# Expert rows filled in rounds, the residual kept on chip, and result gathers ahead of the last routing, in a graph-attention and mixture-of-experts kernel

## The chip, the cores and the metric

The kernel runs on one core of a Trainium2 chip. Its time is the device time of one execution in microseconds (us). Verdicts on two kernels come from runs of both on the same chip.

The engines named below are TensorE (PE; its weight loads are PEld), VectorE (DVE), ScalarE (ACT), GpSimd (POOL) and SyncE (SP). SyncE, ScalarE and GpSimd also issue DMAs; a queue's own instructions have a q behind the name (SPq, ACTq).

## The reference

6250 nodes of 256 values go through a graph-attention layer (8 heads of 32) over 206,250 edges, which are sorted by destination, and then through a mixture of 16 experts of which each node takes two. Both have a residual and a layer norm. Cut to what matters:

```python
h = layernorm(x)
hh = (h @ W).reshape(n, 8, 32)
scores = leaky_relu(s_src[src] + s_dst[dst], 0.2)
alpha = softmax of scores over the edges of one dst
out = segment_sum(hh[src] * alpha, dst) + h
x = x + elu(layernorm(out) * gamma + beta)

y = layernorm(x)
topk_vals, topk_idx = top_k(y @ gate_w + gate_b, 2)
topk_w = softmax(topk_vals)
h = relu(y @ w1[e] + b1[e])
expert_out = h @ w2[e] + b2[e]
moe = sum over the two experts of topk_w * expert_out
x = x + layernorm(y + moe) * gamma + beta
```

## The kernel before

Nodes are handled in 49 blocks of 128. A first stage norms the nodes, multiplies them by W, and writes a table in DRAM with one row of 280 fp32 values a node: 8 heads of 32 values and a one, and the exponentials of its source score. Everything after it happens in one loop, with a tail.

**The edge loop.** The edges are cut into 52 chunks (`k`) of 31 tiles of 128 edges, and each chunk into groups of 8, 8, 8 and 7 tiles (`GROUPS`). For a group:

- GpSimd issues one indirect DMA a tile (`gather`, L188), which fetches the 128 table rows of the tile's sources into a buffer `hx`. The pool has four such buffers, so four groups can be ahead.
- VectorE builds two one-hot matrices of the edges' places among the destinations, `oh` (L864) and `ohT` (L871). TensorE multiplies `ohT` by the destination scores `abw` (L879), into `pm`.
- VectorE folds `pm` (`uv`, L887), multiplies by the source part (L890), takes the larger of two forms (L892) and weighs the rows of `hx` (L895).
- TensorE sums the weighed rows by destination, one product pair a tile (L898), into `agg`. An `hx` buffer is free when its last sum has been made.

At the end of a chunk the last sums are carried into the next (L910, L912) and sent to DRAM (`accd`, L914). SyncE fetches `abw` and the row of places `dlr` two chunks ahead (`fetch`).

**Node blocks.** When a chunk has completed the sums of a block, `node_block` reads them back, norms, applies the elu, adds x, norms again into `acc[:, b, :]`, which stays in SBUF, and computes the gate's logits and their two largest. The residual of the block (`res`, L580) goes out to DRAM (`resd`, L581).

**Parts.** Blocks are gathered into five parts that end at 14, 26, 35, 43 and 49 (`PARTS`). When a part's last block is done, `routing` computes, for each node and each of its two experts, the row in the part's DRAM buffer `xg` at which it stands (`pos`), with each expert's rows filled up to a multiple of 128, and for each tile of 128 rows its expert (`owner`). A part of n blocks needs up to 2n + 15 tiles, 173 in all. GpSimd then scatters the blocks' rows into `xg` (`scatter`, L709), two indirect DMAs a block. `biases` multiplies the routing's shares (`shares`) by the experts' second biases and adds the product to `acc`.

**Expert tiles.** A tile passes through four steps, one a call of `some()`, which is called after each group: `weights` (SyncE reads the expert's number into a register and fetches the tile's rows `xr` L736, `w1s` L738, `b1s` L740), `turned` (fetches `w2s` L745, transposes the rows L749), `hidden` (16 products L758, ReLU on ScalarE L767) and `rows_out` (8 products L773, a copy L775, and a DMA into `yg` L776). `some()` also takes up to four scatters, or one block's biases.

**The tail.** After the last chunk the queues are emptied, and then `result` is called for each block: it gathers its two rows from `yg` (L787, ordered behind the last scatter), adds them with their gates to `acc` (L793), norms, reads the residual back (`res`) and writes the output (L800, L801).

**What sets the order.** The kernel is written with a tile framework, which assigns buffers, adds the waits and places the instructions of each engine in an order of its own making; `tc.issue_after` forces one instruction behind another. On the chip each engine takes its queue in that order. Buffers of a pool are used in turn, and most small products of the parts and of `routing` share one PSUM bank, the tag `pt`.

The lines that call the stages at the end of a chunk:

```python
            for b in when.get(k, ()):
                node_block(b)
                for i, (lo, hi) in enumerate(parts):
                    if b == hi - 1:
                        part_due(i)
```

## Time and profile before

| what | value |
| --- | --- |
| median of 3 runs | 2642.37 us (2632.72 to 2643.17) |
| the profiled execution | 3281.45 us |
| its span, first to last instruction | 3279.4 us |
| TensorE's mean granted clock | 0.796 of full speed |
| first gather's place on GpSimd's queue, last gather | 90.7 us, 2894.0 us |
| bytes read from and written to HBM | 504.0 MB, 86.0 MB |

The profiled execution took 24% longer than the runs that are timed, so durations and gaps in it are those of that execution. A profile gives, for each group of equal instructions, the line, engine, operation, tiles out and in, how often, the busy time and the mean of one, and then how long the engine stood idle just before them and what ended that. Two rows of groups show the form:

```profile
L787 POOL DMA_INDIRECT got<-yg,pos x98 | 97.4, 994 | 197.0 <-DMA yg<-yr 130.7
L767 ACT ACTIVATE hT<-ph,b1s 128x128 f32<-128x128 f32 x692 | 198.1, 368 | 634.3 <-remote 259.3
```

The first says that GpSimd issued 98 result gathers of 0.99 us each, and that it stood idle for 197 us before them, 131 of these until a DMA into `yg` had landed. "remote" means that the event which ended the wait came from no instruction that the profile shows, and "issue" that no wait is shown. Ends of matmuls are modelled.

### The profile page before, as it was taken

Reading aid. Unit: us, or ns where it says so; the run is one execution under the profiler, and the core shown is the slowest. Engines: PE = TensorE matmul, PEld = TensorE weight load, DVE = VectorE, ACT = ScalarE, POOL = GpSimd, SP = SyncE. Lnnn points to the kernel's source line nnn. Section 1 sums busy time; section 2 is a strip of 40 time slices with the busy share of each in tenths; the row PEclk is TensorE's granted clock in tenths of the full one; section 3 lists DMA queues with packets and bytes.
Section 4 is the critical chain, followed back from the end, with each engine's and each line's share of the span. In section 5 each row is a group of like instructions: output and inputs, shape, how many; then the busy total and the mean of one; then the engine's idle time right before and its main releaser. Section 6 shows DMA issues by size and latency. Waiting matters only on the chain. (4 is left out here: it accounts for less than half of the span.)

```text
span 3279.4 us, 34441 instructions
## 1 busy us (share of the span) xinstructions
PE 2002.3 (61%) x10215; PEld 1614.8 (49%) x10215; DVE 1585.7 (48%) x3057; ACT 498.2 (15%) x1771; POOL 1759.4 (54%) x1867
## 2 busy tenths in 40 slices
PE   7344445454424877777636677747677657765565
PEld 5233333343323656666525566645466545654454
DVE  6445555465534444554625456445355524544431
ACT  4000000000000211111101111111111111122232
POOL 3665665666675445655555465664455645515501
PEclk9676777777767888888768888977789868887788
DMA  7875443444443657776546667755576746656896
GB/s 189 249 235 157 119 123 109 121 112 121 120 146 112 198 173 213 224 220 211 150 115 192 184 210 213 231 165 174 161 214 207 216 145 194 200 164 212 259 269 203
DMA packets 415255, 592.51 MB, mean 181 GB/s; under 512 B 104295, under 2 KB 304701, under 8 KB 415061
## 3 DMA queue, kind: packets, MB, share of 16 engines
q1 hardware_dynamic: 268968, 276.81, 28.5%
q0 software_dynamic: 89904, 263.85, 27.8%
q10 hardware_dynamic: 56188, 49.56, 4.4%
q8 instruction: 84, 1.38, 0.2%
q14 instruction: 111, 0.90, 0.1%
HBM read 504.00 MB, written 86.02 MB: 180 GB/s over the span
## 5 line engine op out<-in xcount | busy, mean ns | idle before, releaser
L188 POOL DMA_INDIRECT hx<-table,src_sb x1612 | 1537.3, 954 | 1153.8 <-issue 432.3
L898 PE MATMUL agg<-hx,oh 128*128 128x264 f32 x3224 | 977.3, 462 | 382.1 <-DVE hx L895 222.2
L898 PEld LDWEIGHTS agg<-hx,oh 128*128 128x128 f32 x3224 | 719.8, 231 | 552.1 <-DVE hx L895 233.8
L773 PE MATMUL po<-w2s,hT 128*128 128x256 f32 x1384 | 414.5, 444 | 252.3 <-ACT hT L767 194.6
L887 DVE TENSOR_REDUCE uv<-pm 128x128 f32<-128x384 f32 x208 | 112.2, 539 | 785.2 <-remote 340.0
L895 DVE TENSOR_TENSOR hx<-hx,pm 128x2112 f32<-128x2112 f32 x208 | 474.5, 2281 | 3.4
L773 PEld LDWEIGHTS po<-w2s,hT 128*128 128x128 f32 x1384 | 283.3, 218 | 319.8 <-ACT hT L767 211.9
L758 PEld LDWEIGHTS ph<-xt,w1s 128*128 128x128 f32 x2768 | 368.0, 206 | 44.6 <-issue 27.2
L758 PE MATMUL ph<-xt,w1s 128*128 128x128 f32 x2768 | 377.7, 291 | 12.5 <-issue 7.0
L767 ACT ACTIVATE hT<-ph,b1s 128x128 f32<-128x128 f32 x692 | 198.1, 368 | 634.3 <-remote 259.3
L864 DVE TENSOR_TENSOR oh<-along,dl 128x1024 f32<-128x1024 f32 x208 | 245.3, 1179 | 48.9 <-remote 28.8
L871 DVE TENSOR_TENSOR ohT<-dlr,along 128x1024 bf16<-128x1024 uint8 x208 | 244.8, 1177 | 5.7 <-DMA dlr<-dlb 5.7
L879 PE MATMUL pm<-abw,ohT 128*128 128x48 bf16 x1612 | 88.3, 187 | 237.7 <-DVE ohT L871 143.6
L879 PEld LDWEIGHTS <-ohT 128*128 128x128 bf16 x1612 | 77.4, 99 | 275.7 <-DVE ohT L871 168.6
L787 POOL DMA_INDIRECT got<-yg,pos x98 | 97.4, 994 | 197.0 <-DMA yg<-yr 130.7
L709 POOL DMA_INDIRECT xg<-acc,pos x98 | 96.1, 981 | 94.4 <-DVE pf L689 61.8
L775 ACT COPY yr<-po 128x256 f32<-128x256 f32 x173 | 64.1, 370 | 422.9 <-PE agg L898 107.3
L180 ACT ACTIVATE mv<-mv,eps 128x1 f32<-128x1 f32 x98 | 28.8, 294 | 645.5 <-DVE mv L177 237.4
L589 PE MATMUL pt<-gw,yt 128*128 128x16 f32 x196 | 37.3, 306 | 107.9 <-ACT yt L586 75.0
L727 DVE TENSOR_TENSOR acc<-acc,pt 128x256 f32<-128x256 f32 x49 | 20.5, 418 | 169.9 <-PE pt L726 107.3
L589 PEld LDWEIGHTS pt<-gw,yt 128*128 128x128 f32 x196 | 33.0, 238 | 122.4 <-ACT yt L586 85.6
L793 DVE SCALAR_TENSOR_TENSOR acc<-got,gate,acc 128x256 f32<-128x256 f32 (+1 forms) x98 | 45.3, 474 | 94.2 <-DMA got<-yg,pos 89.2
(185 smaller groups left out, 1314.7 us busy)
## 6 DMA issues: line engine op xcount, KB each, us to landing
w1s<-in_L_ffn_w_dram SPq DMA_DIRECT2D x173, 512.0 KB
w2s<-in_L_ffn_w_dram SPq DMA_DIRECT2D x173, 512.0 KB
hx<-table,src_sb POOLq DMA_INDIRECT x1612
dlr<-dlb SPq DMA_DIRECT2D x52, 496.0 KB
xr<-xg SPq DMA_DIRECT2D x173, 128.0 KB
yg<-yr ACTq DMA_DIRECT2D x173, 128.0 KB
xg<-zero SPq DMA_DIRECT2D x19, 1024.0 KB
accd<-carry ACTq DMA_DIRECT2D x52, 132.0 KB
```

Of the source, the lines that this page charges most:

```text
L188: t = nc.gpsimd.indirect_dma_start(out=hx[:, g, :], out_offset=None, in_=table[:, :], in_offset=bass.IndirectOffsetOnAxis(ap=src_sb[:, c : ...
L709: t = nc.gpsimd.indirect_dma_start(out=xg[i][:, :], out_offset=bass.IndirectOffsetOnAxis(ap=pos[k][:n, b : b + 1], axis=0), in_=acc[:n, b, :],
L758: nc.tensor.matmul(ph[:, f, :], lhsT=w1s[:, k, f * P : (f + 1) * P], rhs=xt[:, k, :], start=(k == 0), stop=(k == KC - 1),)
L767: nc.scalar.activation(hT[:, f, :], ph[:, f, :], AF.Relu, bias=b1s[:, f : f + 1])
L773: nc.tensor.matmul(po, lhsT=hT[:, f, :], rhs=w2s[:, f, :], start=(f == 0), stop=(f == FC - 1))
L787: nc.gpsimd.indirect_dma_start(out=got[:n], out_offset=None, in_=yg[i][:, :], in_offset=bass.IndirectOffsetOnAxis(ap=pos[k][:n, b : b + 1] ...
L864: nc.vector.tensor_tensor(oh, along[:, None, :P].to_broadcast([P, n, P]), dl[:, t0 + g0 : t0 + g0 + n, None].to_broadcast([P, n, P]), ALU. ...
L871: nc.vector.tensor_tensor(ohT, dlr[:, g0 : g0 + n, :], along[:, None, P:].to_broadcast([P, n, P]), ALU.is_equal,)
L879: nc.tensor.matmul(pm[:, g * S3 : (g + 1) * S3], lhsT=ohT[:, g, :], rhs=abw, start=True, stop=True)
L887: nc.vector.tensor_reduce(uv, pm[:, : n * S3].rearrange("p (n t h) -> p n h t", n=n, t=3), AX.X, ALU.add)
L895: nc.vector.tensor_tensor(rows, rows, wt.unsqueeze(3).to_broadcast([P, n, H, D1]), ALU.mult)
L898: nc.tensor.matmul(agg, lhsT=oh[:, g, :], rhs=hx[:, g, :RA], start=(g0 == 0 and g == 0), stop=(carry is None and g0 + g == CT - 1),)
```

## The change

- **Rounds.** The five parts become three rounds, which end at blocks 33, 42 and 49. The first round is routed in seven steps (10, 14, 18, 22, 26, 30, 33). Each step appends to the experts' rows of the round: `count`, `edge`, `here`, `opened` and `whose` carry over from step to step how many rows an expert has, where its open tile lies and which tiles exist. A step makes due the tiles that are full; the last step of a round makes due the rest. A tile's place is no longer its turn, so `page` holds its first row, and SyncE (for `xr`) and ScalarE (for `yg`) read it into a register. There are 81 + 33 + 29 = 143 tiles.
- **Residual.** `rest`, the sum of x and the elu and `fb`, stays in SBUF in place of `acc`, with each block's mean and inverse deviation (`mv2`). `resd` is gone. The rows to scatter are computed again from `rest` just before their scatter (`to_send`), and so is the normed value in `result`.
- **Biases.** `biases` is gone. The shares of all blocks stay in `gives`, with two further columns, and one product in `result` gives the biases, the mean's part and that of `fb`.
- **Order of a group.** `look` makes the one-hots and small products of the next group, ahead of the sums of this one (`issue_after`). Node blocks are called after the first group of the following chunk, and `fetch` after its second. A step's tiles are taken up three groups (`LAG`) after its last scatter.
- **Tail.** After the last gather of the loop, GpSimd gathers the results of the first 12 blocks into three of the four `hx` buffers, ahead of the last routing's scatters; the other blocks follow behind these, four to a buffer. Then each turn of `stages()` is followed by up to two results (four when no tile is left), pinned behind it, and output DMAs follow behind ScalarE's last step.

The diff, cut to its core:

```diff
+LAG = 3
-PARTS = (14, 26, 35, 43, 49)
+ROUNDS = ((10, 14, 18, 22, 26, 30, 33), (42,), (49,))
...
+    PAGES = [2 * (hi - lo) + E - 1 for lo, hi in zip(begins, ends)]
+    for r, cuts in enumerate(ROUNDS):
+        lo, done = begins[r], 0
+        for hi in cuts:
+            n = PAGES[r] if hi == cuts[-1] else max(0, 2 * (hi - begins[r]) - E + 1)
+            parts.append((lo, hi, r, hi == cuts[-1], n - done))
+            lo, done = hi, n
...
 def node_block(b):
-            y = acc[:, b, :]
+            y = w2_.tile([P, C], F32, name="y")
             nc.vector.tensor_scalar(y, xb, mv[:, 0:1], mv[:, 1:2], op0=ALU.subtract, op1=ALU.mult)
-            nc.vector.tensor_add(res, xb, fb)
-            nc.scalar.dma_start(resd[b * P : (b + 1) * P, :], res)
+            nc.vector.tensor_add(rest[:, b, :], xb, fb)
...
 def routing(i):
+                nc.vector.tensor_tensor(place, place, count[:, None, :].to_broadcast([P, nb, E]), ALU.add)
+            nc.vector.tensor_add(count, count, incl[:, nb - 1, :])
+            nc.vector.tensor_sub(over, count, edge)
...
+                pr = wk.tile([P, 1], F32, name="pt")
+                nc.tensor.matmul(pr, lhsT=tri, rhs=due_now, start=True, stop=True)
+                nc.vector.tensor_copy(rank, pr)
+                nc.vector.tensor_scalar(take, irow[:, :mt], rank, due_now, op0=ALU.is_equal, op1=ALU.mult)
...
+                pp = wk.tile([1, mt], F32, name="pt")
+                nc.tensor.matmul(pp, lhsT=first_row, rhs=take, start=True, stop=True)
+                nc.vector.tensor_copy(page[i], pp)
...
+            po = wk.tile([1, mt], F32, name="pt")
+            nc.tensor.matmul(po, lhsT=whose, rhs=take, start=True, stop=True)
+            marks["dve"] = nc.vector.tensor_scalar_min(owner[i], po, float(E - 1))
...
+        def to_send(b):
+            y = e2.tile([P, C], F32, name="ys", bufs=7)
+            nc.vector.scalar_tensor_tensor(
+                y, rest[:, b, :], mv2[:, b, 0:1], fb, op0=ALU.subtract, op1=ALU.subtract
+            )
+            nc.scalar.activation(y, y, AF.Copy, scale=mv2[:, b, 1:2])
+            return y
...
-        def biases(i, b):
-            nc.tensor.transpose(pt, shares[i][:, b - parts[i][0], :], ident)
-            nc.scalar.copy(gt, pt)
-            nc.tensor.matmul(pb, lhsT=gt, rhs=b2r, start=True, stop=True)
-            nc.vector.tensor_add(acc[:, b, :], acc[:, b, :], pb)
...
 def weights(i, j):
+            if parts[i][-1] < PAGES[r]:
+                row = load(page[i][:, j : j + 1], 0, (PAGES[r] - 1) * P, engines=(ET.SP,), after=after)
-            nc.sync.dma_start(xr, xg[i][j * P : (j + 1) * P, :])
+            t = nc.sync.dma_start(xr, xg[r][ds(row, P), :])
...
 def rows_out(i, j, w2s, hT):
+            if parts[i][-1] < PAGES[r]:
+                row = load(
+                    page[i][:, j : j + 1], 0, (PAGES[r] - 1) * P, engines=(ET.Activation,), after=stored[-1:]
+                )
+            t = nc.scalar.dma_start(yg[r][ds(row, P), :], yr)
...
+        def result(i, b, got):
+            pt = wps.tile([E + 2, P], F32, name="agg")
+            nc.tensor.transpose(pt, gives[:, b, :], ident)
+            nc.scalar.copy(gt, pt)
+            pb = wps.tile([P, C], F32, name="pm")
+            nc.tensor.matmul(pb, lhsT=gt, rhs=b2r, start=True, stop=True)
+            nc.vector.scalar_tensor_tensor(y, rest[:, b, :], mv2[:, b, 1:2], pb, op0=ALU.mult, op1=ALU.add)
...
+        def look(k, i):
+                if len(weighed) > 0:
+                    order.enter_context(tc.issue_after(weighed[-1].ins))
+                ohT = w3_.tile([P, n, P], BF16, name="ohT")
+                oh = w3_.tile([P, n, P], F32, name="oh")
+            pm = wps.tile([P, n * (S3 + H)], F32, name="pm")
+                if sums:
+                    order.enter_context(tc.issue_after(sums[-1].ins))
+                for g in range(n):
+                    t = nc.tensor.matmul(
+                        pm[:, g * S3 : (g + 1) * S3], lhsT=ohT[:, g, :], rhs=abw, start=True, stop=True
+                    )
...
+                with tc.issue_after(looked.ins):
+                    for g in range(n):
+                        t = nc.tensor.matmul(
+                            agg,
...
                 some()
+                if g0 == 0:
+                    blocks(summed)
+                    summed = []
+                elif g0 == GROUPS[0] and k + 2 < NK:
+                    fetch(k + 2)
...
+        for _ in range(3):
+            fetch_set(gathered)
+        blocks(summed)
+        scatters(len(scat))
+        while sets or got or due or any(at) or outs:
+            stages()
...
+            while outs and (len(outs) > 2 or not got):
+                with tc.issue_after(marks["act"].ins):
+                    result_out(*outs.popleft())
+            for _ in range(2 if left else 4):
...
+                    outs.append(result(i, b, rows))
...
+            while sets and held < 4 and not any(open_tiles(i) for i, _ in sets[0]):
+                fetch_set(scattered[-1][-1][1])
+                held += 1
```

## The prediction

> **What bounds the kernel now.** I read the page's busy lines first, then the costliest groups, then stretches of 82 us, then the waits of GpSimd, then one stretch of the timeline where engines stand idle together, and last the chain of waits, which covers only the end.
>
> The page's busy line and three of its groups (busy us, mean ns; then idle before them and what ended it):
>
> ```profile
> PE 2002.3 (61%) x10215; PEld 1614.8 (49%) x10215; DVE 1585.7 (48%) x3057; ACT 498.2 (15%) x1771; POOL 1759.4 (54%) x1867
> ...
> L188 POOL DMA_INDIRECT hx<-table,src_sb x1612 | 1537.3, 954 | 1153.8 <-issue 432.3
> ...
> L773 PE MATMUL po<-w2s,hT 128*128 128x256 f32 x1384 | 414.5, 444 | 252.3 <-ACT hT L767 194.6
> ...
> L709 POOL DMA_INDIRECT xg<-acc,pos x98 | 96.1, 981 | 94.4 <-DVE pf L689 61.8
> ```
>
> No engine is full. The longest serial resource is GpSimd's queue: each of the 1612 gathers takes 0.95 us and is followed by 0.30 us of "issue", so one goes every 1.25 us and the 31 of a chunk cost 38.75 us; all take 2015 us. The stretches (length; busy us and count of PE, PEld, DVE, ACT, POOL; clock; DMA share; GB/s):
>
> ```profile
> 574.00:656.00 82.00, 35.69 (x172) 27.93 (x170) 37.45 (x65) 3.41 (x11) 50.57 (x54) 0.71 0.44 121
> ...
> 902.00:984.00 82.00, 22.50 (x96) 17.04 (x96) 30.83 (x85) 3.94 (x13) 60.37 (x63) 0.62 0.50 146
> ...
> 1394.00:1476.00 82.00, 63.67 (x346) 52.05 (x345) 48.85 (x82) 15.28 (x51) 48.69 (x52) 0.90 0.75 220
> ...
> 3116.00:3198.00 82.00, 56.01 (x303) 45.78 (x302) 29.00 (x80) 28.29 (x108) 3.49 (x4) 0.90 0.92 268
> ```
>
> 54 gathers in 82 us are 47 us a chunk, 52 are 48.9: about 9 us a chunk over the pace, with experts beside the edges (1394) or without (574). In 902 to 984 stand the first part's 28 scatters; that chunk took 97 us from one first weighting (L895) to the next, and the other three routed chunks 91, 103 and 94. The chunks after a routing take 61 to 68, where the part's bias products are dealt out. From the first gather's place at 90.7 to the last at 2894.0 are 2803 us; gathers and the 86 scatters at 1.265 us (109) leave 679 us in which GpSimd could have gone on. What ended its waits:
>
> ```profile
> POOL hx L188 <- PE agg L898: 181.3, 28, 16.9
> POOL hx L188 <- PE pm L879: 164.8, 30, 18.1
> POOL hx L188 <- remote: 110.3, 41, 5.1
> POOL hx L188 <- PE ph L758: 97.5, 23, 19.8
> ```
>
> So it waits for one of the four hx buffers, which TensorE has not summed yet. Why TensorE is late, in the timeline (start, length):
>
> ```profile
> 541.75 0.61 PE L910 MATMUL agg<-carry,shift 128*128 128x264 f32 x2
> ...
> 542.19 0.36 PE L879 MATMUL pm<-abw,ohT 128*128 128x48 bf16 x8
> ...
> 552.45 0.38 ACT L912 COPY carry<-agg 128x264 f32<-128x264 f32 x1 [17.12 <-remote]
> ...
> 560.22 0.56 DVE L887 TENSOR_REDUCE uv<-pm 128x128 f32<-128x384 f32 x1 [17.92 <-issue]
> ```
>
> The products end by 542.6 in the record; their readers start 10 and 18 us later, with nothing else ahead of them. TensorE then waits for VectorE, so its lateness comes round again. The tail, in the chain:
>
> ```profile
> 3198.68 1.80 PE ph L758 x16
> 3200.93 1.13 PE po L773 x4
> ...
> 3203.14 1.80 PE ph L758 x16
> 3205.39 1.13 PE po L773 x4
> ```
>
> One expert tile each 4.46 us when nothing disturbs it.
>
> **What the Trainium skill says.** "Perfetto Trace Analysis", Tensor Engine Instruction: a matmul's end is estimated, and the semaphore goes out only when PSUM has acknowledged. The 10 and 18 us above agree that a matmul's row does not tell when its reader may go. "TensorE: Matmul & The Clock Gate", What's actually happening: the array falls to half clock after an idle window and needs a busy one to come back. The trace agrees: clock 0.71 where TensorE has gaps, 0.90 in 1394 to 1476. "DMA: Bandwidth & Descriptors", Issuing engines are not separate DMA queues: all queues share the same engines; the last stretch agrees (share 0.92 at 268 GB/s with all three queues active).
>
> **The change, part by part** (sum against the profiled execution: 3281 us, its span of 3279.4 and 2 around it).
>
> *Order of the edge loop.* In the built order before, an expert's second product often stands close behind its ReLU (po waits 194.6 us for hT), small products come in runs of 15, and the node block's transposes stand ahead of the last sum, waiting for VectorE. Afterwards each group is: next group's products, 8 sums, then po of one tile, hidden of the next, transposes of a third. VectorE can then weigh the next group while TensorE sums. Needs of a chunk: TensorE 62 sums at 0.222 us apart (13.8) + 4 tiles at 4.46 (17.8) + some 3 = 35; VectorE 4 x (2 x 1.21 + 0.55 + 0.28 + 0.23 + 2.35) = 23 + 5.5 for a node block; bytes 4.4 MB of gathers + 5.1 of tiles + 1.2, 10.7 MB, at 268 GB/s 40 us. GpSimd's 38.75 + 2 for scatters is the longest, just. Four buffers are 39 us of gathers; landing, weighing and summing one takes some 20 to 30, so about 10 us of lateness is absorbed. I take half of 8.5 us a chunk as left: 4.3 x 52 = 220. Bounds: nothing left (0), or all (440).
>
> *Routings.* Eight instead of four stand inside the loop. Before, each cost 97 - 48, 43, 55 and 46 us over a plain chunk, of which 28, 24, 18 and 16 scatters are 35, 30, 23 and 20 of GpSimd: stalls of 14, 13, 32 and 26, mean 21. A routing now has some 25 more small VectorE instructions (0.2 us each, 5 us) and three more TensorE products through the one pt bank, but most are followed by 8 scatters, not 16 to 28. I take 10 us each, 80; bounds 0 and 60. Sum of idle afterwards 300, for 679 now: -379. Scatters in the loop fall by two (nothing).
>
> *Biases and residual.* 43 bias products leave the loop (ACT 0.26, VectorE 0.42, TensorE 1.37 us each): their share of the three slow chunks, about 139 us in all, is inside the 679. They return in the tail in psum banks that are free there. The residual's 98 DMAs (12.8 MB, 0.33 us of ScalarE issue each) go. Row sends cost one VectorE pass (0.48) and one ScalarE copy (0.37) per block, spread: nothing. Reading the page number costs ScalarE and SyncE some 0.5 us on 81 tiles, on engines busy 15%: nothing; uncovered it would be 40.
>
> *Tiles.* 143 for 173: 30 x 4.46 = 134 us of TensorE and 38 MB, but the built order still leaves 45 for after the last edge sum, 42 before. So this relieves the loop (2 tiles a chunk up to chunk 38) and not the tail.
>
> *Tail.* 385 us from the last gather. Its 61.8 us wait for the last routing now holds 24 result gathers (30 us). Of 45 stages some 23 carry two results: 4.46 + 2 x 1.37 = 7.2; 166 + 22 x 4.46 = 264. Bytes: 45 x 1.28 + 49 x 0.13 out + 37 x 0.26 got = 74 MB, 275 us at 268 GB/s: that governs. With 41 before the stages and 31 from the last tile's store to the end (3248 to 3279): 345, -40. Bounds -90 and +20.
>
> Sum: 3281 - 379 - 40 = 2862.
>
> **To the median.** The runs shown take 2642, 639 less than the profiled one, and the trace doesn't say where. If everything shrinks alike (x 0.805), the gain is 337: 2305. If the excess sits wholly in the waits, 40 us of the 679 remain to be won, 22 of them at the same share (379/679), and the tail's 32: 2588. I take half of the 679: 340 x 0.56 = 190, + 32: **2420**.
>
> **Rivals.**
> - *Nearly all waits go* (for it: four buffers of slack and a fixed order; against: the late signals are no dependency that the order removes): idle 150, 529 + 50 less, at 0.805: about 2190.
> - *Gathers already pace the unprofiled run* (for: 90.7 + 2124 + 385 x 0.805 = 2525 lies near 2642 if a gather takes 1.25 there too): 2580.
> - *Slower by the routings*: each has five products in a row through one bank, every one with in-order TensorE, VectorE and ScalarE behind it, and GpSimd behind the positions. Price before: 21 us with two products. It decides from about 62 us each: 8 x 62 = 496 - 85 = 411, which eats the 419. At 75 us (+105, x 0.805): 2727. Against: TensorE's slack of 4 us a chunk or more, and less to do in each.
> - *No change*, the stalls only moving: 2642.
>
> **How the numbers follow.** Chances: 0.50 for 2420 (own range 2300 to 2530), 0.20 for 2190, 0.18 for 2580, 0.09 slower, 0.03 none. Range 2210 to 2600: the low end just past the second case, the high end past the third. 0.5% is 13 us, about what this measurement can tell: faster 0.87, same 0.04, slower 0.09.
>
> **What would show it.** POOL counts of 60 or more in 82 us instead of 52 to 54; waits of hx for PE under 300 us; clock over 0.85; po's wait for hT gone; chunks with a routing under 65 us; w1s issued 143 times; result gathers ahead of the last 14 scatters; ACT's resd lines gone. Wrong would be: GpSimd waiting for pos tens of us at eight places, or chunks still at 47 us with nothing but late signals in them.

## The result, and the profile after

The changed kernel takes 2608.83 us (median of 4 runs, 2607.0 to 2611.91), the kernel before 2640.33 us beside it; the ratio is 0.9886, with a 95% interval of 0.9862 to 0.991. That is faster by 1.1%, some 30 us, where 220 had been forecast.

One thing has to be known to read the numbers: the first profiled execution of the kernel before (3281 us) and two later groups of runs fell into stretches in which every kernel took some 450 to 650 us longer than at other times, called drawn-out here; ratios are always taken within one group of runs on one chip.

Only when the kernel before was run and profiled again (first experiment) was there a trace of it that is like the timed runs. Its span is 2635.0 us. Its busy line and the row of the gathers on its page (the line number is one higher, for a constant that was added):

```profile
PE 1893.2 (72%) x10215; PEld 1554.9 (59%) x10215; DVE 1584.5 (60%) x3057; ACT 495.7 (19%) x1771; POOL 1764.5 (67%) x1867
...
L189 POOL DMA_INDIRECT hx<-table,src_sb x1612 | 1542.4, 957 | 541.8 <-issue 432.7
```

And the same two lines of the changed kernel's page (span 2606.2 us):

```profile
PE 1770.8 (68%) x9497; PEld 1467.4 (56%) x9497; DVE 1636.2 (63%) x3483; ACT 465.4 (18%) x1652; POOL 1763.9 (68%) x1866
...
L200 POOL DMA_INDIRECT hx<-table,src_sb x1612 | 1542.5, 957 | 544.0 <-issue 429.3
```

The gather rows are the same: 1542 us busy and 542 or 544 us idle, nearly all of it the 0.3 us of "issue" behind each gather. The 1154 us of idle time that the first profile showed in this row had not been there in a timed run. The stretches of 82 us say the same. Of the kernel before (columns: length; busy us and count of PE, PEld, DVE, ACT, POOL; clock; DMA share; GB/s):

```profile
410.00:492.00 82.00, 50.83 (x211) 38.86 (x212) 55.12 (x92) 4.74 (x15) 62.20 (x66) 0.80 0.51 141
...
2050.00:2132.00 82.00, 64.26 (x350) 53.39 (x349) 49.95 (x105) 15.37 (x53) 61.19 (x64) 0.85 0.75 236
2460.00:2542.00 82.00, 56.55 (x302) 47.89 (x303) 37.09 (x103) 29.50 (x114) 13.78 (x15) 0.88 0.91 283
```

Of the changed kernel:

```profile
410.00:492.00 82.00, 48.71 (x202) 37.91 (x202) 53.53 (x93) 5.65 (x18) 62.20 (x66) 0.77 0.49 137
...
2050.00:2132.00 82.00, 49.95 (x266) 41.72 (x267) 41.73 (x85) 12.23 (x40) 62.19 (x66) 0.79 0.66 204
2460.00:2542.00 82.00, 74.83 (x473) 64.18 (x472) 18.49 (x52) 35.84 (x124) 0.00 (x0) 1.00 0.94 293
```

In the loop's two stretches GpSimd issues 64 to 66 instructions in 82 us in both: 82 / 1.25 is 65.6, so the gathers stand all but back to back before the change already. Over the loop's other stretches (from 164 to 2214 us) the counts are 59 to 67 before and 60 to 67 after. The last line is the tail: there TensorE goes from 302 to 473 products.

The starts of the gathers and the last instruction, taken from the traces, split the time. "Idle" is what the spaces between the starts of GpSimd's instructions in the loop have beyond 1.25 us, summed.

| kernel | first to last gather | idle | last gather to the end |
| --- | --- | --- | --- |
| before | 2191 us | 70 us | 351 us |
| changed | 2190 us | 72 us | 324 us |
| before, first profile | 2801 us | 680 us | 385 us |

So the loop as a whole didn't gain, and the tail's 27 us are the gain. Two questions follow: why the loop stayed where it was to the microsecond though so much in it was changed, and which of the tail's edits won the 27 us.

### The profile page after: what moved, and what is told of

The parts are those of the page before. It is cut to its first block, busy times and chain, and to the rows that moved or that the text cites. A ratio compares the mean times of both kernels' runs of the same rounds, so it can differ in the third digit from the quotient of the medians.

```text
span 2606.2 us, 33384 instructions
## 1 busy us (share of the span) xinstructions
PE 1770.8 (68%) x9497; PEld 1467.4 (56%) x9497; DVE 1636.2 (63%) x3483; ACT 465.4 (18%) x1652; POOL 1763.9 (68%) x1866
## 4 chain that ended last, share of the span: by engine, by line
PE 26%; POOL 24%; DMA 19%; DVE 15%; issue 13%; ACT 2%; DVEq 0%; POOLq 0%; ACTq 0%; SPq 0%
POOL hx L200 23%; PE agg L1063 11%; DMA hx<-table,src_sb 9%; PE ph L868 5%; PE po L883 5%; DVE hx L1059 5%; DMA out_dram<-o 3%; DMA accd<-carry 2%; DMA xg<-ys,pos 2%; PE ph L291 2%; POOL xg L817 1%; DMA a<-accd 1%; DVE oh L1016 1%; DVE s L188 1%; DVE uv L1054 1%
## 5 line engine op out<-in xcount | busy, mean ns | idle before, releaser
L1059 DVE TENSOR_TENSOR hx<-hx,pm 128x2112 f32<-128x2112 f32 x208 | 474.5, 2281 | 3.9
L883 PE MATMUL po<-w2s,hT 128*128 128x256 f32 x1144 | 289.9, 393 | 45.8 <-ACT hT L877 45.4
L868 PEld LDWEIGHTS ph<-xt,w1s 128*128 128x128 f32 x2288 | 287.4, 196 | 20.6 <-issue 7.6
L868 PE MATMUL ph<-xt,w1s 128*128 128x128 f32 x2288 | 292.4, 281 | 3.5 <-DMA w1s<-in_L_ffn_w_dram 2.5
L1054 DVE TENSOR_TENSOR uv<-uv,hx 128x128 f32<-128x128 f32 x208 | 59.9, 288 | 340.1 <-DMA hx<-table,src_sb 287.2
L883 PEld LDWEIGHTS po<-w2s,hT 128*128 128x128 f32 x1144 | 218.2, 196 | 89.4 <-ACT hT L877 59.2
L902 POOL DMA_INDIRECT hx<-yg,pos x98 | 97.1, 991 | 168.8 <-DVE y L920 117.3
L859 PE MATMUL pt<-ident,xr 128*128 128x128 f32 x286 | 58.0, 286 | 165.6 <-DMA xr<-xg 164.9
L859 PEld LDWEIGHTS pt<-ident,xr 128*128 128x128 f32 x286 | 38.0, 149 | 174.4 <-issue 159.5
L817 POOL DMA_INDIRECT xg<-ys,pos x98 | 96.2, 981 | 55.1 <-issue 49.0
L861 ACT COPY xt<-pt 128x256 f32<-128x256 f32 x143 | 54.9, 384 | 320.4 <-PE pt L859 313.5
```

Source lines behind the costliest of these rows:

```text
L817: t = nc.gpsimd.indirect_dma_start(out=xg[r][:, :], out_offset=bass.IndirectOffsetOnAxis(ap=pos[k][:n, b : b + 1], axis=0), in_=sent_rows[ ...
L868: marks["pe"] = nc.tensor.matmul(ph[:, f, :], lhsT=w1s[:, k, f * P : (f + 1) * P], rhs=xt[:, k, :], start=(k == 0), stop=(k == KC - 1),)
L883: marks["pe"] = nc.tensor.matmul(po, lhsT=hT[:, f, :], rhs=w2s[:, f, :], start=(f == 0), stop=(f == FC - 1))
L902: t = nc.gpsimd.indirect_dma_start(out=into[:n, k, :C], out_offset=None, in_=yg[parts[i][2]][:, :], in_offset=bass.IndirectOffsetOnAxis(ap ...
L1059: nc.vector.tensor_tensor(rows, rows, wt.unsqueeze(3).to_broadcast([P, n, H, D1]), ALU.mult)
```

## The experiments

Eighteen runs. The theory behind the first four (A) is that gathers pace the timed runs; the rivals are that idle time was there as well and was lost to new waits. Later texts name their own theories.

### The kernel before once more

One unused constant is added, which changes no instruction.

> The kernel before, unchanged, profiled a second time. Theory A (the gathers on GpSimd pace both kernels in the timed runs, and the first trace of before was drawn out by something that timed runs lack): a time near 2640 us, and if the profile is not drawn out, a span near it with less than 150 us of GpSimd idle beyond one gather every 1.25 us in the loop. Theory B (before waits for TensorE in timed runs as in its trace, and the gain of the change is lost again elsewhere): over 350 us of such idle also in a trace whose span is near 2640.

2636.7 us (16 runs, ratio 1.0006, 0.9994 to 1.0019), profile 2637 us. Its table row and stretches stand above: 59 to 67 instructions of GpSimd in 82 us of the loop, where the prediction had read 52 to 54 in stretches without scatters. A sum over its waits shows another mark: no wait in it is put down to "remote", where the first profile has 1262 us of such waits. What was read off the first profile as room was the property of that execution. Of its own 70 us of idle time the largest part is this one of its waits:

```profile
POOL hx L189 <- PE pt L585: 44.2, 20, 4.8
```

Twenty times a gather's wait, of up to 4.8 us, ends with the transposes of a node block (L585) on TensorE.

### Half the gathers

Every second gather is left out in both kernels, and with it half of the edges' rows; the pool of buffers becomes four fixed ones, zeroed once. The output isn't the reference's.

```diff
-        for g in range(n):
+        for g in range(0, n, 2):
```

> The kernel before with every second gather left out (806 of 1612; those rows of the buffers stay zero, so half of the edges are not summed; the products and VectorE's passes stay). Theory A: with 1008 us less for GpSimd the time falls by more than 300 us, below 2340, to where TensorE's and VectorE's chain holds it. Theory B: that chain holds it already, so it falls by less than 150 us, above 2490.

> The changed kernel with every second gather left out in the same way. Theory A: below 2200 us, since the other engines need some 33 to 36 us a chunk (92 + 52 x 33 + 324 = 2130), and further below e2 than the two whole kernels are apart, because the new order counts once gathers don't pace. Theory B: above 2450 us.

Before 2333.99 us (ratio 0.8862, 0.8844 to 0.888), changed 2072.67 us (0.787, 0.7852 to 0.7888): 261 us apart, where the whole kernels are 30 apart. From the first to the last gather it is 1884 and 1638 us, so 246 of the 261 lie in the loop. What the change does to the loop is real and large, and it is hidden by the gathers: taking 780 of them off wins 302 us before and 536 after. There are only two runs of each, and the gathers' bytes go with them; that it is GpSimd's queue that paces, and not the bytes, is read from the pace itself: in the changed kernel 66 instructions stand in 82 us both at a DMA share of 0.49 (410 to 492 us) and at 0.88 (1886 to 1968 us). Which of the edits to the loop win the 246 us was not taken apart.

### The changed kernel without its order

The look-ahead is undone and its three constraints are dropped or put back as in the kernel before; the rest of the change stays, the later place of the node blocks too.

```diff
-                if len(weighed) > 0:
-                    order.enter_context(tc.issue_after(weighed[-1].ins))
+                if len(weighed) > 1:
+                    order.enter_context(tc.issue_after(weighed[-2].ins))
...
-                if sums:
-                    order.enter_context(tc.issue_after(sums[-1].ins))
...
-                oh, pm, looked = looks.popleft()
-                if len(weighed) + 1 < NK * len(GROUPS):
-                    looks.append(look(*divmod(len(weighed) + 1, len(GROUPS))))
-                    looked = looks[-1][-1]
+                oh, pm, looked = look(*divmod(len(weighed), len(GROUPS)))
...
-                with tc.issue_after(looked.ins):
+                with ExitStack() as order:
```

> The changed kernel with one part undone: the one-hots and small products of a group are made in the group's own turn and not a group ahead, with the order constraints of before. Theory A: the order is hidden by the gathers, 2590 to 2640 us. Theory B: the order is what the loop gained, 2700 us or more.

2611.65 us (ratio 0.9915, 0.9896 to 0.9934). Loop 2204 us, idle 85, tail 318. The look-ahead alone is worth some 13 us in the loop, in a single profile, and nothing that can be told in the whole.

### The residual's trip put back

```diff
+    resd = dram.tile([NB * P, C], F32, name="resd")
...
+            nc.scalar.dma_start(resd[b * P : (b + 1) * P, :], rest[:, b, :])
...
+            res = e2.tile([P, C], F32, name="res")
+            nc.scalar.dma_start(res, resd[b * P : (b + 1) * P, :])
```

The last step of `result` reads `res` for `rest`, and the pool `ys` has five buffers for seven, to make room.

> The changed kernel with the residual's trip through memory put back: each node block stores its 128 KB in the loop and each result loads them in the tail (6.4 MB more after the last gather). Theory 'bytes set the tail': before moved 89 MB after its last gather in 351 us, the changed kernel 82.5 MB in 324 us, 254 and 255 GB/s; the 6.4 MB come back as about 25 us, 2634, nearly the whole gain. Rival 'stages of tiles and results on TensorE set the tail': nothing, 2609 to 2612. Rival 'the result gathers ahead of the last routing are the gain': nothing, 2609. In the loop, where GpSimd's gathers pace, the stores cost nothing in any of them.

2634.23 us (13 runs, ratio 0.9999, 0.9987 to 1.0011): the gain is gone, some 25 us, and all of it in the tail, 349 us for 324. (The changed kernel was not run beside this one, nor beside the runs with half the weights, with the gathers behind and with the earlier rounds. Its ratio is 0.9886 in one group of runs and 0.9907 in another, so a difference to it across groups is sure to some 6 us.) The next kernel keeps the stores and the loads, but each load brings only 8 rows of 128, into the place in `rest` where they stand already, so that the tile `res` goes:

```diff
+            nc.scalar.dma_start(rest[:8, b, :], resd[b * P : b * P + 8, :])
```

> As the run with the residual's trip put back (2634), but each result loads only 8 of its 128 rows, into the place where they stand already; the 49 stores in the loop, the 49 load instructions on ScalarE's queue, the wait for them and the five buffers for rows stay. Theory 'bytes': 0.4 MB instead of 6.4 MB in the tail, so the 25 us go again: 2609 to 2614. Rival 'issue and waits on ScalarE's queue, or the two buffers of rows less': stays at 2630 to 2637.

This run and the three beside it fell into a drawn-out stretch (the kernel before at 3249 us, the median of the runs that the ratio uses): 3075.88 us, ratio 0.9465 (0.9423 to 0.9507), which doesn't answer the question. So it was run again:

> As put on record for the run with 8 rows: theory 'bytes' 2609 to 2614; rival 'issue and waits on ScalarE's queue, or the two buffers of rows less' 2630 to 2637. In a session with late signals: within 10 us of the changed kernel under 'bytes', 25 above it under the rival.

2614.39 us (ratio 0.9923, 0.9905 to 0.9941), beside the changed kernel unchanged on the same chip:

> The changed kernel unchanged, as the base of the other three. Where gathers pace (before at 2635): 2609, loop 2190 and tail 324. In a session with late signals (before at 3252): between 3065 and 3090, as the four variants had 3071 to 3097; the fall then sits in the loop (679 us of GpSimd's idle time beyond its pace before, 460 to 510 in the variants), which is the size of gain that the prediction's idle term meant.

2609.21 us (ratio 0.9907, 0.9884 to 0.993). So of the trip's 25 us some 20 go with its bytes, and up to 5 with its instructions, waits and the buffers; the intervals of the last two ratios overlap, so these 5 are not told from nothing. Stretches of the tail of the changed kernel, where tiles and results run together (first two) and where tiles run alone (last):

```profile
2365.00:2410.00 45.00, 39.55 (x204) 32.19 (x204) 33.72 (x94) 20.73 (x82) 34.46 (x35) 0.89 0.97 324
2410.00:2455.00 45.00, 39.19 (x230) 31.75 (x228) 35.81 (x101) 21.59 (x85) 17.44 (x18) 1.00 0.95 308
2500.00:2545.00 45.00, 41.20 (x270) 36.60 (x269) 0.00 (x0) 18.89 (x61) 0.00 (x0) 1.00 0.93 296
```

The same stretches with the trip put back:

```profile
2365.00:2410.00 45.00, 38.70 (x172) 30.24 (x171) 25.27 (x69) 16.30 (x65) 30.39 (x32) 0.77 0.95 306
2410.00:2455.00 45.00, 38.21 (x203) 29.23 (x201) 31.94 (x88) 18.13 (x76) 11.82 (x13) 0.92 0.94 306
2500.00:2545.00 45.00, 38.98 (x244) 34.21 (x243) 5.87 (x16) 17.31 (x59) 0.00 (x0) 0.96 0.90 281
```

The DMA engines are busy 94 to 97% of the first two stretches in both, and the extra bytes push products out: 375 for 434. The granted clock is lower there too, 0.77 for 0.89 and 0.92 for 1.00, and TensorE's busy time falls by only 1 us in each. With 8 rows loaded they are 425 products, at a clock of 0.96 in both. Fewer bytes and a higher clock went together, and no run has one without the other; what a product at the lower clock adds to the bytes is not shown. By the starts of the tiles' second products a stage (one tile and two results) takes 6.4 us in the changed kernel, 7.4 with the trip and 7.2 in the kernel before.

### Half the weights

Every second tile takes the weights of the tile before, so the weights of 71 tiles, 1 MB each, are left out. The output isn't the reference's.

```diff
-            w1s = e2.tile([P, KC, F], F32, name="w1s")
-            nc.sync.dma_start(w1s, w1[ds(e, 1)].rearrange("a (k p) f -> p (a k) f", p=P))
+            if len(kept1) % 2 == 0:
+                w1s = e2.tile([P, KC, F], F32, name="w1s")
+                nc.sync.dma_start(w1s, w1[ds(e, 1)].rearrange("a (k p) f -> p (a k) f", p=P))
+            else:
+                w1s = kept1[-1]
...
+            if len(kept2) % 2 == 0:
+                w2s = e2.tile([P, FC, C], F32, name="w2s")
```

> The changed kernel where every second expert tile loads no weights and takes those of the tile before it; the loads of 71 of the 143 tiles' weights (1 MB each) are left out, so the output is not the reference's. In the tail 22 or 23 of 45 tiles bring no weights, 23 MB less of 82. Theory 'bytes set the tail': at 255 GB/s 90 us less, until 4.46 us of TensorE a tile stop it: 45 x 4.46 + 41 before + 31 after = 273 for 324, so 2558. Theory 'stages on TensorE set the tail' (a tile at 4.3 to 4.5 us, with two results 6.3): at most 5 us less, 2604 to 2609. The loop is paced by GpSimd in both and stays at 2190 us.

2584.59 us (ratio 0.9812, 0.9791 to 0.9833): 24 us less than the changed kernel's 2609 (20 to 25 by the ratios), with 24 MB less in the tail. Neither theory has it right alone. The same three stretches as above:

```profile
2365.00:2410.00 45.00, 43.20 (x255) 35.07 (x253) 39.48 (x111) 23.80 (x94) 32.96 (x33) 1.00 0.87 286
2410.00:2455.00 45.00, 43.90 (x256) 35.78 (x257) 40.97 (x115) 25.74 (x100) 17.44 (x18) 1.00 0.76 241
2500.00:2545.00 45.00, 42.32 (x279) 37.67 (x277) 0.00 (x0) 18.37 (x62) 0.00 (x0) 1.00 0.55 175
```

With the bytes gone TensorE is busy 43 to 44 of 45 us. A stage with results falls from 6.4 to 5.7 us and stops there; a tile alone falls from 4.4 to 4.2 only. So where results run beside tiles the bytes set the pace, with TensorE some 0.7 us a stage behind, and where tiles run alone TensorE does.

### The result gathers behind the last scatters

```diff
-        for _ in range(3):
-            fetch_set(gathered)
         blocks(summed)
         scatters(len(scat))
+        for _ in range(3):
+            fetch_set(scattered[-1][-1][1])
```

> The changed kernel with the first 24 result gathers placed behind the last 14 scatters, as the kernel before has all of its result gathers. Theory 'the gathers ahead are the gain': 24 gathers at 1.25 us = 30 us back, 2639. Theory 'bytes set the tail': same bytes, but the first 20 us of results move from before the last scatters to later stages; 2609 to 2619. Theory 'stages set the tail': results still end before the last tile, so 2609 to 2615.

2625.62 us (ratio 0.9967, 0.9954 to 0.998): 16 to 21 us back by the two ratios of the changed kernel, rather more than half of the 30 that the 24 gathers take. Having them ahead is the second part of the tail's gain. With the residual's 25 and three tiles more in the tail at 4.4 us (13), 25 + 16 - 13 = 28, for the 27 measured. That these add was not tested, nor what the tail's other edits (results pinned behind stages, the biases' product) do.

### The empty stretch at the last routing

The timeline of the changed kernel shows that from 2312 to 2340 us little but the last routing runs, while some 12 tiles that are due stand behind it in program order. First an attempt to shorten the tail by cutting the rounds earlier, which leaves fewer tiles, and so fewer to cover this stretch with:

```diff
-ROUNDS = ((10, 14, 18, 22, 26, 30, 33), (42,), (49,))
+ROUNDS = ((10, 14, 18, 22, 26, 29, 31), (39,), (49,))
```

> The changed kernel with its rounds cut earlier: steps at blocks 10, 14, 18, 22, 26, 29, 31, then 39, then 49, for 10 to 33, then 42, then 49; 143 tiles in both, but the built order leaves 36 instead of 45 behind the last edge sum, and the last round has 10 blocks for 7. If the loop is paced by gathers alone the 9 tiles cost nothing there. In the tail they save 9 x 4.4 = 40 us of stages, or 9 x 1.28 = 11.5 MB = 45 us of bytes; three more results behind the last tile give 6 gathers and about 10 us back. So 2575 to 2580 under both; if the last routing and the results fix the end, 2605 or more.

2603.69 us (ratio 0.9887, 0.9868 to 0.9906): 0 to 5 us less for nine tiles less, where 29 to 34 were expected. The gap between two tiles' last products at the last routing grew from 37 to 76 us, which fits a stretch in which no tile was left to run. That led to the reverse, tiles put into the stretch:

```diff
-        blocks(summed)
+        for b in summed:
+            stages()
+            stages()
+            node_block(b)
+        for _ in range(4):
+            stages()
+        part_due(len(parts) - 1)
         scatters(len(scat))
```

> The changed kernel with tiles of the round before placed ahead of, between and behind the last two node blocks, instead of behind the last routing. Now from 2312 to 2339 us nothing is moved and TensorE does only the node blocks' small products, while some 12 tiles that are due stand behind them. Theory 'the tail is stages, by TensorE or by bytes, plus this empty stretch': 6 tiles of 4.3 us fit into it, so 20 to 27 us less than 2609: 2582 to 2589. Rival 'the last routing sets the end': its products now stand behind tiles, the last scatters come 10 to 20 us later and so does the end: 2610 to 2630.

> The same filling with the rounds cut earlier (10, 14, 18, 22, 26, 29, 31; 40; 49), which leaves 41 tiles behind the last edge sum instead of 45, nine node blocks in the last round instead of seven, and about 8 due tiles to fill the empty stretch with. Theory 'stages plus empty stretch': 4 x 4.3 = 17 us less, two more results behind the last tile 6 us back: about 10 below the run with the filling alone, 2572 to 2580. Rival 'too few tiles are left to cover the last routing': the same as the filling alone or above, 2585 to 2605.

Both fell into the drawn-out stretch: 3070.53 us (ratio 0.9461, 0.9424 to 0.9498) and, with earlier rounds, 3089.04 us (0.9517, 0.9482 to 0.9552); the second has a gap of 69 us between two tiles again, and is not faster than the first, as its rival said. The filling was run again:

> As put on record for the filled stretch: theory 'stages plus the empty stretch' 2582 to 2589, 20 to 27 us below the changed kernel; rival 'the last routing sets the end' 2610 to 2630.

2594.07 us (ratio 0.9852, 0.9832 to 0.9873), 15 us below the changed kernel. The stretch before (changed kernel):

```profile
2312.00:2340.00 28.00, 6.62 (x22) 4.35 (x22) 18.26 (x85) 5.87 (x20) 2.12 (x3) 0.54 0.22 72
```

and with the filling:

```profile
2312.00:2340.00 28.00, 18.23 (x98) 15.07 (x96) 12.39 (x45) 10.41 (x35) 0.48 (x1) 0.82 0.65 207
```

The last scatter comes 23 us later, and the end still comes 15 us earlier: the last routing doesn't set the end; how much is left to run behind it counts. The expected 20 to 27 were not reached; a gap of 15 us between tiles that is still in the stretch fits that.

### Five plain rounds

The rounds of the kernel before, 173 tiles, in the changed kernel; `ys` has five buffers.

```diff
-ROUNDS = ((10, 14, 18, 22, 26, 30, 33), (42,), (49,))
+ROUNDS = ((14,), (26,), (35,), (43,), (49,))
```

> The changed kernel with five plain rounds as in the kernel before (14, 26, 35, 43, 49; 173 tiles instead of 143, four routings in the loop instead of eight, five buffers for rows instead of seven); the built order leaves 46 tiles behind the last edge sum instead of 45. Theory 'gathers pace the loop': the 30 tiles (38 MB, 134 us of TensorE) cost nothing there and the fewer routings give back up to 4 x 6 us minus what larger ones cost; loop 2180 to 2195, whole 2600 to 2615. Rival 'the rounds are part of the gain': 134 us of TensorE shared over the loop, 2630 or more.

In the drawn-out stretch 3097.34 us (ratio 0.9549, 0.9513 to 0.9585), the slowest of the four there. Again:

> As put on record for the five plain rounds: theory 'gathers pace the loop' 2600 to 2615 (loop 2180 to 2195); rival 'the rounds are part of the gain' 2630 or more. In a session with late signals the loop is not paced by gathers, and the 30 tiles more may cost there: 3097 against 3071 to 3089 of the three others says 10 to 25 us.

2588.08 us (ratio 0.9825, 0.9804 to 0.9845): 21 us below the changed kernel, and below both of what the theories had said. Its loop is 2159 us with 37 us idle, its tail 327. So the other edits to the loop had won 33 us of the 70 after all, and the rounds in steps gave them back. What was won has the size of the wait for the node blocks' transposes: of its 44 us before, the plain rounds have nothing left, the changed kernel 0.3 us, and that kernel without the look-ahead 0.6. That fits the later place of the node blocks, which all three have; no run has this place alone undone. The five buffers are not what took the stalls away: the runs with the residual's trip have five as well, and keep them (loop 2192 us). Where the rounds gave it back, the list of long spaces between GpSimd's instructions shows: besides one near 131 us, which both have, the changed kernel has six spaces over 2 us, of 4.6 to 6.7 us beyond the pace, 37 us in all, one at each of the first round's seven steps but the earliest; the plain rounds have none. The first of the six in the timeline of the changed kernel (start, length, and in brackets the idle time before):

```profile
862.96 0.96 POOL L817 DMA_INDIRECT xg<-ys,pos  x1 [0.30 <-issue]
864.22 0.98 POOL L200 DMA_INDIRECT hx<-table,src_sb  x1 [0.30 <-issue]
865.40 0.34 SPq L842 DMA_DIRECT2D xr<-xg  x1
...
867.63 0.66 PE L859 MATMUL pt<-ident,xr 128*128 128x128 f32 x2 [27.58 <-DMA xr<-xg]
...
868.09 3.20 PE L1063 MATMUL agg<-hx,oh 128*128 128x264 f32 x8
...
871.56 0.96 POOL L200 DMA_INDIRECT hx<-table,src_sb  x1 [6.36 <-PE agg L1063]
```

Read from the bottom: GpSimd waits 6.4 us for sums; the sums stood behind the transposes of a tile's rows, at which TensorE had waited 27.6 us, though VectorE had weighed the rows to be summed by 842.1; the tile's rows were fetched when the step's last scatter was out (863); and the eight scatters had stood in GpSimd's queue behind more than ten gathers. The gathers in four buffers take 39 us, and of the 27.6 us 6.4 reach GpSimd. In the waits of the changed kernel:

```profile
PE pt L859 <- DMA xr<-xg: 164.9, 7, 28.2
POOL hx L200 <- PE agg L1063: 59.8, 90, 6.9
```

and with five plain rounds, where TensorE has no such wait:

```profile
POOL hx L200 <- PE agg L1063: 21.0, 69, 0.3
...
ACT hT L877 <- DMA xr<-xg: 9.8, 17, 1.4
```

### A step's tiles two groups later

```diff
-LAG = 3
+LAG = 5
```

> The changed kernel with LAG 5 for 3: a step's first tile starts five groups after its last scatter was put in the program instead of three, some 20 us later. Theory 'TensorE stands in order at rows that are still on their way, and its sums behind it hold up the gathers': the waits for xr fall from 165 us to below 40, the six stalls (37 us) go, the loop falls from 2190 to 2155 to 2160; the built order leaves 47 tiles for 45 in the tail, 9 us back: 2578 to 2588. Rival 'the stalls are VectorE's, in the routing's many small instructions': they stay, and the two tiles add 9: 2615 to 2620.

> The same with the stretch at the last routing filled with tiles as well (15 us by the run of the filling alone): 2563 to 2573 if both gains add; as the run with LAG 5 alone, or above it, if the later tiles take each other's place.

Both fell into the second drawn-out stretch (the kernel before at 3277 us): 3121.9 us (ratio 0.9524, 0.9473 to 0.9575), and 3099.54 us with the filling (0.9452, 0.9408 to 0.9496). In the waits of the first:

```profile
POOL hx L200 <- PE agg L1063: 208.8, 43, 13.9
...
PE pt L859 <- DMA xr<-xg: 9.4, 3, 8.4
```

The wait for the rows is short, as the first theory has it. But the 165 us are not what to compare with: the run with the filling alone, drawn-out too and with `LAG` at 3, has this:

```profile
PE pt L859 <- DMA xr<-xg: 35.8, 7, 10.5
```

And with the filling, the longer `LAG` wins nothing that can be told (ratio 0.9452 against 0.9461). In such a stretch other waits of TensorE hold the gathers up, so the loop doesn't show what the edit is worth where gathers pace. That the stalls come from this wait rests on the timeline and on the plain rounds; that a longer `LAG` wins them back stays open.

The fastest kernel that leaves nothing out is the changed one with five plain rounds, 0.9825 of the kernel before and, by the medians of one group of runs, 2588 to 2609 us against the changed one. The filling (0.9852) is a separate gain of 15 us in the tail; the two together were not run.

## Why the prediction was wrong

The direction was right and the size was not. The step that failed is "To the median". It had a profiled execution of 3281 us for runs of 2642 and took half of GpSimd's 679 us of idle time, 340 us, to be there in a timed run, of which 190 would be won. By the second profile of the kernel before, nearly all of the excess of 639 us sat in that idle time: the loop's idle time is 70 us for 680, and the tail 351 for 385; these two, 610 and 34, make the 644 us by which the two spans differ. The lateness of 10 and 18 us, which the prediction took for that of any execution, belongs there too: before the fold of `pm` (L887) VectorE is idle for 785 us in the first profile and for 179 in the second. The prediction had written this case down ("if the excess sits wholly in the waits, 40 us of the 679 remain": 2588) and weighed it as the far end. Its third case, that gathers already pace the unprofiled run, gave 2580 and is the one that happened, for 2609 measured; its one argument, 90.7 + 2124 + 310 = 2525 near 2642, was the only view of the profile that tied the trace to the timed runs, and it deserved more than 0.18. (Two of its sums are off without bearing on this: 41 + 275 + 31 is 347 and not 345, and 579 us at 0.805 give 2176 and not 2190.)

Point by point:

- *A gather every 1.25 us.* Right: the median distance of two is 1.25 us in every trace, drawn-out ones too, and 2015 us of the loop's 2190 are this.
- *Idle time of 300 us left of 679 (220 by the order, 80 by eight routings).* Mis-sized. In the drawn-out stretches, where the step can be compared with a trace like the one it was read from, six variants of the changed kernel have 461 to 513 us idle (the one with 8 rows 461) and are 4.5 to 5.5% faster than before, not 13%. Where gathers pace, order and the loop's other edits win 33 us (five plain rounds), about the size of the waits for the node blocks' transposes, which the prediction had named, and six stalls of 6 us give 37 back.
- *What a routing costs.* The forecast looked for it in VectorE's small instructions, the `pt` bank and GpSimd waiting for positions. It lies at the tile behind the step: TensorE waits 27 us at rows whose scatters are still behind gathers. The size, 10 us at each of eight, was near: six stalls of some 6 us.
- *Biases and residual.* The residual has no term of its own in the sum; that it is gone stands only, unnamed, in the tail's 74 MB. The stores in the loop cost nothing; the 6.4 MB of loads in the tail cost 25 us, some 20 of them going with the bytes. It is the largest single part of the gain. The prediction's own sentence that bytes govern the tail would have given it: 6.4 MB at its 268 GB/s are 24 us. What the biases' move is worth no run shows.
- *Tiles, 30 less, no gain in the tail.* Right in sign: the built order leaves 45 for 42, and the loop has room for all 173, as the plain rounds show. In the drawn-out stretch, where TensorE holds the gathers up, the rounds are 21 us faster than the plain ones by the nearest pair (3076 with 8 rows loaded, 3097 plain; the intervals of their ratios just miss each other); where gathers pace, they are 21 us slower. Fewer tiles were worth nothing there because TensorE's load wasn't what the loop waited for.
- *Tail, -40.* Nearly right in size (-27, and -31 in the second profile of the changed kernel), but in part by luck: gathers ahead were put at 30 and gave 16 to 21, the residual's share was not seen as such, and that bytes govern holds only for the stages with results. The rate was put at 268 GB/s; it is 308 to 324 there, and the 385 us from which the 40 were taken belong to the drawn-out execution (351 in the second profile).
- *Slower by the routings*, from 62 us a routing on: the stalls are a tenth of that.

What the prediction said would show it: 60 and more instructions of GpSimd in 82 us, waits of `hx` for TensorE under 300 us and `w1s` 143 times all came true, but the first two were so in the kernel before as well, as soon as it was not drawn out. They were marks of the execution, not of the change. Three other signs did not come: the clock is 0.831 and not over 0.85 (it was 0.855 before, in the second profile), `po` still waits 45 us for `hT`, and five of the changed kernel's chunks take 66 to 68 us by their first weightings, not under 65.

## What to carry to other kernels

When a profiled execution is far from the timed runs, first find the resource whose pace alone accounts for the timed runs (here 1612 gathers at 1.25 us, and what lies before and behind), and lay the excess on the waits of that resource until another profile says otherwise; "remote" as the releaser of many waits was the mark of such an execution. In a kernel whose loop one queue paces, edits are worth what they do to the few waits of that queue and to the stretches outside the loop: count the tail's bytes by tensor, and look there for times in which no engine but one runs. And a tile taken up behind its scatters stands, in order, in front of everything that its engine does next: how far behind is decided by what the scatters' own queue has ahead of them.

## What the runs showed of the hardware that was not expected

- The same program takes 2633 to 2640 us by the medians of four groups of runs and 3249 and 3277 in two others, there in all of the group's runs and in all its kernels; one chip showed both at different times. The first profiled execution took 3281 us beside timed runs of 2633 to 2643. Instructions of GpSimd and VectorE last as long as ever (a gather 952 to 958 ns, a weighting 2281 or 2282); TensorE's are longer in part, at a lower granted clock (a product of `po` 444 ns at 0.796 in the first profile of the kernel before, 403 at 0.855 in the second). What is longer besides is the time from a product's end in the record to its reader's start, as in the prediction's timeline. Two lines from the waits of the run with 8 rows loaded, drawn-out:

```profile
DVE uv L1054 <- remote: 322.7, 44, 14.9
ACT yt L614 <- remote: 239.3, 20, 22.0
```

Waits put down to "remote" sum to 1262 to 1659 us in the seven drawn-out traces and to none in the thirteen others. What lies behind it is not shown.

- GpSimd's indirect gather of 128 rows costs 0.95 us and 0.30 us until the next, in every trace, and at DMA shares from 0.49 to 0.88; leaving out 780 of them is worth up to 536 us.
- The tail of the changed kernel moves 308 to 324 GB/s over 45 us at a DMA share of 0.95 to 0.97 (323 to 336 in its second profile), well above the 268 that the first profile showed at 0.92. The kernel before has it too where its result gathers run: 322 GB/s at 0.97 (2378 to 2460 us of its second profile).
